# Port-aware ordering of an attention front, residual norms moved to ScalarE, and half sums, in a cross-attention and expert-FFN kernel

## The chip, the cores and the metric

The kernel runs on one core of one Trainium2 chip. The metric is the device time of one launch in microseconds; the shown time is the median of three runs. A profile of one execution comes with it. Engines are named as the profile names them: PE is TensorE, PEld its weight loads, DVE is VectorE, ACT is ScalarE, POOL is GpSimd and SP is SyncE, which here only issues DMAs.

## The reference, cut to what matters

Sixteen sequences of 112 tokens and 256 features (x) attend to sixteen contexts of 375 rows (ctx), all in float32. After the attention's residual comes a mixture of eight experts in which every token goes through every expert.

```python
x = x + xattn(layernorm(x), ctx, Wq, bq, Wk, bk, Wv, bv)
x = x + ffn(layernorm(x), w_router, w_gating, w_gate, w_up, w_down)

def xattn(t, c, ...):                       # one head, 256 wide
    q, k, v = t @ Wq + bq, c @ Wk + bk, c @ Wv + bv
    return softmax(q @ k.T / 16) @ v

def ffn(h, ...):                            # 8 experts, 256 -> 1024 -> 256
    cw = softmax(h @ w_router) * softmax(h @ w_gating / 0.1)
    cw = cw / (cw.sum(-1) + 1e-9)
    return sum(cw[e] * ((silu(h @ w_gate[e]) * (h @ w_up[e])) @ w_down[e]) for e in range(8))
```

## The kernel before, in words

**The front.** x arrives in four groups of four batches (`load_x`), ctx batch by batch (`load_ctx`). Wq and Wk are joined into one 256 by 256 matrix (`turned`, `joined`), and the biases are folded in as a column `r_sb`, a row `v_b` and a number `bqk_b` (`dotted`, L711, and `key_bias`, L720). For that, bq, bk and bv are loaded as rows repeated over 128 partitions (`row`, L627), and bk once more as columns (`columns`, L631), which VectorE widens into `bkb` (L730). Each group of x is normed (`stats` L751 and L752, a power on GpSimd at L759, `norm` at L771 or L776), transposed and multiplied with the joined matrix.

Each of the sixteen batches then runs a chain (`batch`): transposes of ctx (L846) and their copies out of PSUM (L853), scores (L858), maximum and shift (L866, L869), exponential (L873), transposes of the probabilities (L879) and copy (L884), mix of ctx rows (L892), a split into a high and a low part (L898, L901), projection by Wv (L907), residual (L914), then statistics of the new row x1 (L930 to L932), a power on GpSimd (L936), the residual norm x1n on VectorE (L942), its transposes (L950) and the copy into x1T (L957). When x1T of a half (eight batches, h = 0 or 1) is there, the router's logits follow (`route`, L978 to L1018), and the blocks that the FFN's products need.

**The FFN.** A step is an expert, a half of the tokens, one of four column blocks and gate or up: 128 steps. Each product of 2 x 2 blocks is made with seven block products instead of eight (`PROD`), each in three passes over high and low parts of both operands. So each half of x1T is needed as A11, A12, A22 and the sums S1 to S4 (`sum_x`, L256, on VectorE), each split by ScalarE into a rounded part (`split_hi`, L264) and by GpSimd or VectorE into the rest (`split_lo`, L267). The sums of both halves use the same buffer `sx`. The weights go the same way: `load_t` on GpSimd (L301 to L304), `load_hi` on ScalarE (L316), `load_lo` on GpSimd (L322). The down products (L383) fill gaps between block products (L417).

**What sets the order.** The engines run their instructions in the order of emission. For the front that order comes from a list, class `Line`: each operation is given with its engine, an assumed cost, a priority, what it reads and writes, and the buffers it takes. `run` simulates the engines by these costs, always takes the operation that can begin first (among equal ones the one of lower priority number), and emits all in the order of the simulated times. An operation is bound to one engine, and the list knows nothing of engines that hinder each other. The FFN's steps are written out by hand (`step`), with places where waiting pieces may be put in (`offer`). For h = 1 the four sums and five splits are such pieces, put into steps 1 to 3 by `sums_later`, two of the five rests on VectorE; the routing of h = 1 lies wholly in the list. Before the first data arrive, `idle` issues `WARM` = 11 matmuls on zeros.

**Memory.** Buffers of the FFN (`buf`) lie in one pool in the order of their first use; all have sizes that are multiples of 256 bytes.

Of the kernel before, what the change touches and what calls it, by code (L numbers as in the profile page):

```python
# [30 lines left out]
class Line:  # L31


    LAG = {"PE": 0.2, "SP": 0.1}

# [8 lines left out]
    def op(self, eng, cost, pri, emit, reads=(), writes=(), new=(), waits=(), kb=0):  # L44
        n = len(self.ops)
        deps = set()
        for k in reads:
            deps.update(self.writers[k])
        for k in waits:
            deps.update(self.uses[k])  # L50
        writes = tuple(writes) + tuple(x[1] for x in new)
        for k in tuple(reads) + writes:
            self.uses.setdefault(k, []).append(n)
        for k in writes:
            self.writers.setdefault(k, []).append(n)
        self.ops.append((eng, cost, pri, emit, deps, tuple(new), kb))
        return n

    def run(self):
        ops = self.ops  # L60
        end = {}
        free = {}
# [25 lines left out]
        while left:  # L88
            ready = {}
            for n in left:  # L90
                eng, cost, pri, emit, deps, new, kb = ops[n]
                if any(d not in end for d in deps):
                    continue
                t = max((end[d] + (0.0 if ops[d][0] == eng else self.LAG.get(ops[d][0], 0.1)) for d in deps), default=0.0)
                homes = {}
                for ring, key, *tag in new:
                    r, home = room(ring, tag[0] if tag else None, max(t, free.get(eng, 0.0)) - 0.1)
                    if r is None:
                        t = None
                        break  # L100
                    t = max(t, r + 0.1 if r else r)
                    homes[key] = home
                if t is not None:
                    ready.setdefault(eng, []).append((t, pri, n, homes))
            best = None
            for eng, c in ready.items():
                at = max(free.get(eng, 0.0), min(x[0] for x in c))
                x = min((x for x in c if x[0] <= at + 0.02), key=lambda x: (x[1], x[2]))
                if best is None or at < best[0]:
                    best = (at, eng, x)  # L110
            assert best, [(n, ops[n][0], ops[n][5]) for n in sorted(left) if all(d in end for d in ops[n][4])]
            at, eng, (_, _, n, homes) = best
            cost, kb, new = ops[n][1], ops[n][6], ops[n][5]
# [3 lines left out]
            free[eng] = at + cost  # L117
            end[n] = at + cost
# [5 lines left out]
        for at, n in sorted(line):  # L124
            ops[n][3]()
# [4 lines left out]
def kernel(  # L130
# [63 lines left out]

    def buf(tag, shape, name, dtype=F32):
        return fpool.tile(shape, dtype, tag=tag, name=name, bufs=BUFS[tag])
# [9 lines left out]
    nc.scalar.activation(warm, nhalf, AF.Exp)  # L206
# [33 lines left out]
    bk_c = spool.tile([P, KC], F32, tag="bk_c", name="bk_c", bufs=1)  # L240
    junk = cpool.tile([P, D], F32, name="junk")
# [6 lines left out]
    def sum_x(h, i):  # L248

        a11, a12, a21, a22 = blocks_of_x(h, 0, N)  # L250
        s1, s2, s3, s4 = (sx[:, k, :] for k in range(4))
        o, u, v, op = {
            X_S1: (s1, a21, a22, ALU.add), X_S2: (s2, s1, a11, ALU.subtract),
            X_S3: (s3, a11, a21, ALU.subtract), X_S4: (s4, a12, s2, ALU.subtract),
        }[i]
        nc.vector.tensor_tensor(o, u, v, op=op)  # L256

    def block_x(h, i):
        a11, a12, a21, a22 = blocks_of_x(h, 0, N)
        blocks = {X_A11: a11, X_A12: a12, X_A22: a22}  # L260
        return blocks[i] if i in blocks else sx[:, i - X_S1, :]

    def split_hi(h, i):
        nc.scalar.copy(xs_hi[h][i], block_x(h, i))  # L264

    def split_lo(h, i, eng):
        eng.tensor_sub(xs_lo[h][i], block_x(h, i), f(xs_hi[h][i]))  # L267
# [336 lines left out]

    def bank(key, shape):
# [14 lines left out]
    rsx, nmx, rs1, cs = (many(n, B) for n in ("rsx", "nmx", "rs1", "cs"))  # L620
# [5 lines left out]
    def row(t, v):  # L626
        nc.sync.dma_start(t, v.rearrange("(o d) -> o d", o=1).to_broadcast([P, D]))  # L627

    def columns():
        with nc.allow_non_contiguous_dma(reason="bias columns"):  # L630
            nc.sync.dma_start(bk_c, bk.rearrange("(c p) -> p c", p=P))  # L631
# [17 lines left out]

    def x_loaded(g):  # L650
        op("SP", 0.45, 4 * g - 6 if g else -22, lambda: load_x(g), new=(("xg", ("xg", g)),), kb=448)
# [4 lines left out]
    WARM = 11  # L656
# [9 lines left out]
    load(-18, 256, lambda: weight(nc.sync, wn[:, 1], Wk), "wn1")  # L666
    ctx_loaded(0)
    load(-3.2, 128, lambda: row(b_b[:, 0], bq), "bq")
    load(-3.1, 1, columns, "bkc")
    load(-3.0, 128, lambda: row(b_b[:, 1], bk), "bk")  # L670
    load(-2.0, 128, lambda: row(bv_b, bv), "bv")
    load(-1.7, 256, lambda: weight(nc.sync, wv, Wv), "wv")
    load(1.0, 16, load_router, "wr")
    for b in range(1, B):
        ctx_loaded(b)
    for g in range(1, B // G):
        x_loaded(g)

# [30 lines left out]
    def dotted(u, v, out, key, *reads):  # L709
# [6 lines left out]
        op("DVE", 0.52, -4, dot, reads=reads, writes=(key,))  # L716
# [11 lines left out]
    for i in range(KC):  # L728
        joined(i)
    op("DVE", 0.3, -8, lambda: nc.vector.tensor_copy(bkb, bk_c.unsqueeze(2).to_broadcast([P, KC, P])),  # L730
       reads=("bkc",), writes=("bkb",))
# [11 lines left out]
    def group(g):  # L743
# [10 lines left out]
        for i in range(G):  # L754
            op("DVE", 0.62, pri, lambda i=i: stats(i), reads=(("xg", g),), writes=(("st", g),))
        op("DVE", 0.18, pri, lambda: nc.vector.tensor_scalar_add(rsx[:TQ, at], mvx[:TQ, at, 1], EPS),
           reads=(("st", g),), writes=(("va", g),))
        op("POOL", 1.04, pri,
           lambda: nc.gpsimd.tensor_tensor(rsx[:TQ, at], rsx[:TQ, at], nhalf[:TQ, :G], op=ALU.pow),  # L759
           reads=(("va", g),), writes=(("rs", g),))  # L760
        op("DVE", 0.22, pri,
           lambda: nc.vector.scalar_tensor_tensor(
               nmx[:TQ, at], mvx[:TQ, at, 0], -1.0, rsx[:TQ, at], op0=ALU.mult, op1=ALU.mult),
           reads=(("rs", g),), writes=(("nm", g),))
# [16 lines left out]
        for i in range(G):  # L781
            key = ("xn", g, i // 2)
            op("DVE" if g == 0 and i % 2 else "ACT", 0.43, pri, lambda i=i: norm(i), reads=(("nm", g), ("xg", g)) + ((key,) if i % 2 else (("xnd", g if i else g - 1),) if g + i else ()),
               writes=((key,) if i % 2 else ()) + (("xnd", g),), new=(() if i % 2 else (("tt", key),)))
# [12 lines left out]
        for k in range(KC):  # L797
            op("PE", 0.4, pri, lambda k=k: turn(k), reads=(("xn", g, 0), ("xn", g, 1)),
               new=(("bank", ("xT", g, k)),))
            op("ACT", 0.54, pri, lambda k=k: nc.scalar.copy(xnT_b[k], bank(("xT", g, k), [P, GT])),  # L800
# [25 lines left out]
        for i in range(G):  # L826
            op("DVE", 0.52, pri + 0.5, lambda i=i: bias(i), reads=(("xn", g, i // 2), "v"), writes=(("c0", g),))
# [4 lines left out]
    def batch(b):  # L832
# [18 lines left out]
        for k in range(KC):  # L851
            op("PE", 0.33, b + 0.6, lambda k=k: turn(k), reads=(("ctx", b),), new=(("bank", ("cT", b, k)),))
            op("ACT", 0.45, b + 0.6, lambda k=k: nc.scalar.copy(ctT(k), bank(("cT", b, k), [P, TK])),  # L853
               reads=(("cT", b, k),), new=(("ctT", ("ctT", b, k)),))

        def score():
# [14 lines left out]
           reads=(("mx", b), ("c", g)), writes=(("nb", b),))  # L871
# [12 lines left out]
        op("ACT", 0.45, b, lambda: nc.scalar.copy(pT(), bank(("pp", b), [KT, NK, TQ])),  # L884
# [13 lines left out]
        op("ACT", 0.36, b, lambda: nc.scalar.copy(aT()[:, 0], bank(("aa", b), [P, KC, TQ])),  # L898
# [30 lines left out]
        def stats():  # L929
            nc.vector.bn_stats(st1[:TQ, b, :], x1())  # L930
            nc.vector.bn_aggr(mv1[:TQ, b, :], st1[:TQ, b, :])
            nc.vector.tensor_scalar_add(rs1[:TQ, col], mv1[:TQ, b, 1:2], EPS)  # L932

        op("DVE", 0.8, b, stats, reads=(("x1", b),), writes=(("va1", b),))
# [5 lines left out]
        def norm():  # L940
            t[0] = buf("y", [TQ, D], f"x1n{b}")
            nc.vector.tensor_scalar(  # L942
                t[0], x1(), mv1[:TQ, b, 0:1], rs1[:TQ, col], op0=ALU.subtract, op1=ALU.mult
            )

        op("DVE", 0.42, b, norm, reads=(("x1", b), ("rs1", b)), new=(("x1n", ("x1n", b)),))

        def turn_x1():
# [7 lines left out]
        op("ACT", 0.36, b,  # L956
           lambda: nc.scalar.copy(x1T[h][:, :, at * TQ : (at + 1) * TQ], bank(("xx", b), [P, KC, TQ])),  # L957
# [6 lines left out]

    lgs = [spool.tile([P, NTT, 2, E], F32, tag=f"lg{h}", name=f"lg{h}", bufs=1) for h in range(NH)]
# [4 lines left out]
    def route(h):  # L970
# [50 lines left out]

        op("DVE", 0.5, pri + 12, sums, reads=(("le", h),), writes=(("w1", h),))
# [4 lines left out]
    def split(h, i, pri, *reads):  # L1027
        op("ACT", 0.57, pri, lambda: split_hi(h, i), reads=reads, writes=(("xh", h, i),))
        op("POOL", 1.12, pri, lambda: split_lo(h, i, GP), reads=(("xh", h, i),) + reads, writes=(("xs", h, i),))
# [7 lines left out]
    for n, i in enumerate((X_S1, X_S2, X_S3, X_S4)):  # L1037
        op("DVE", 0.63, 9.5 + 0.1 * n, lambda i=i: sum_x(0, i),
           reads=early(0) + late(0) + [("sx", k) for k in (X_S1, X_S2, X_S3, X_S4)[:n]], writes=(("sx", i),))
    for i in (X_S2, X_S1, X_S3, X_A22, X_S4):  # L1040
        split(0, i, 10.5, *late(0), *([("sx", i)] if i != X_A22 else []))
    route(1)

# [90 lines left out]
    def sums_later():  # L1134
        for i in (X_S1, X_S2, X_S3, X_S4):
            sum_x(1, i)
            yield
        for i in (X_S2, X_S1, X_S3, X_A22, X_S4):
            split_hi(1, i)
            yield  # L1140
            split_lo(1, i, V if i in (X_S1, X_S2) else GP)
            yield

    for n in range(1, len(steps)):
        if n == 1:
            waiting.append(sums_later())
        assert not (waiting and n == 4)
        step(n)
    KEEP = 0
# [42 lines left out]
```

## Time and profile before

| | |
|---|---|
| median of 3 runs | 1007.76 us (1007.69 to 1008.76) |
| profiled execution | 1007.49 us, span 1005.7 us, 16283 instructions |
| busy PE, PEld | 981.5 us (98%), 911.1 us (91%) |
| busy DVE, ACT, POOL | 807.0 us (80%), 497.9 us (50%), 416.0 us (41%) |
| mean granted TensorE clock | 0.993 |
| DMA | 39.06 MB, mean 39 GB/s; 236 GB/s in the first 40 us |

The span is the time from the program's first to its last instruction; the execution's own time is some 2 us longer. A busy TensorE is not one at its peak, since its matmuls are pipelined. Windows of the span are counted in microseconds from its start.

### The profile page before, as it was taken

The numbers are of one execution on the slowest core, as the hardware profiler recorded it, in microseconds if no ns is written. First come the engines' busy times: TensorE is split into PE (matmuls) and PEld (weight loads), VectorE is DVE, ScalarE is ACT, GpSimd is POOL, SyncE is SP. The second block draws the span as 40 slices with busy tenths as digits, with TensorE's granted clock in tenths as the row PEclk, the third lists the DMA queues.
The fourth block names the chain that finished last, engine by engine and source line by source line (L and its number), as shares of the span: only waits on it lengthen the run. The fifth ranks groups of instructions, "written<-read, shape, count | busy, mean of one in ns | idle before, by whom it ended". The sixth has DMA issues, their size and how long they took to land.

```text
span 1005.7 us, 16283 instructions
## 1 busy us (share of the span) xinstructions
PE 981.5 (98%) x6055; PEld 911.1 (91%) x6055; DVE 807.0 (80%) x1481; ACT 497.9 (50%) x1017; POOL 416.0 (41%) x516
## 2 busy tenths in 40 slices
PE   8998879999999999999999999999999999999998
PEld 5777868999999999999999999999999999999998
DVE  6686689878878888878887887888887888788786
ACT  5565365445535554545544553555444544455342
POOL 4354456244605552356324460555235632455000
PEclk9998999999999999999999999999999999999999
DMA  8610101001100110011100110011001110010011
GB/s 233 184 55 21 45 22 53 22 23 43 53 1 22 43 42 22 11 43 42 34 11 23 43 53 1 22 43 43 22 12 42 43 32 11 22 43 1 1 37 37
DMA packets 36735, 39.06 MB, mean 39 GB/s; under 512 B 3552, under 2 KB 34656, under 8 KB 36656
## 3 DMA queue, kind: packets, MB, share of 16 engines
q1 hardware_dynamic: 36384, 37.76, 12.7%
q8 instruction: 47, 0.77, 0.3%
q14 instruction: 32, 0.26, 0.1%
q10 hardware_dynamic: 272, 0.26, 0.1%
HBM read 34.34 MB, written 1.84 MB: 36 GB/s over the span
## 4 chain that ended last, share of the span: by engine, by line
PE 91%; DVE 4%; DMA 2%; issue 1%; POOL 1%; ACT 0%; DVEq 0%; POOLq 0%; ACTq 0%
PE pd L383 31%; PE pC L417 15%; PE pA L417 15%; PE pB L417 15%; PE pE L417 7%; PE ps_aa L892 2%; PE ps_sc L858 2%; DMA ctx<-in_ctx_dram 1%; DVE x1n L942 1%; PE ps_po L907 1%; PE ps_cT L846 1%; PE ps_pp L879 0%; DMA wide<-in_x_dram 0%; PE ps_lg L978 0%; POOL rs L936 0%
## 5 line engine op out<-in xcount | busy, mean ns | idle before, releaser
L383 PE MATMUL pd<-wd,hhi 128*128 128x256 f32 x1792 | 340.7, 281 | 0.0
L383 PEld LDWEIGHTS pd<-wd,hhi 128*128 128x128 f32 x1792 | 309.6, 188 | 15.0
L383 PE MATMUL pd<-wd,hlo 128*128 128x256 f32 x896 | 253.1, 283 | 1.3 <-DVE hlo L470 0.7
L417 PE MATMUL pC<-xs_hi,w 128*128 128x448 f32 x508 | 188.6, 371 | 2.9 <-DVE s_4c L551 1.2
L417 PE MATMUL pB<-xs_hi,w 128*128 128x448 f32 x508 | 187.1, 368 | 2.7 <-DVE s_1w L528 2.7
L417 PE MATMUL pA<-xs_hi,w 128*128 128x448 f32 x504 | 186.8, 371 | 0.6 <-ACT v L523 0.6
L383 PEld LDWEIGHTS pd<-wd,hlo 128*128 128x128 f32 x896 | 169.5, 189 | 1.7 <-DVE hlo L470 0.9
L400 POOL TENSOR_TENSOR acc<-acc,y 128x256 f32<-128x256 f32 x45 | 36.0, 828 | 250.1 <-ACT y L399 250.1
L322 POOL TENSOR_TENSOR w<-raw,w 128x384 fp32r<-128x384 f32 x64 | 73.0, 1140 | 148.7 <-ACT w L316 148.7
L523 ACT COPY v<-pA 128x448 f32<-128x448 f32 x126 | 67.0, 532 | 91.6 <-PE pA L417 91.6
L417 PEld LDWEIGHTS pC<-xs_hi,w 128*128 128x128 f32 x508 | 96.1, 189 | 12.5 <-DVE s_4c L551 1.4
L417 PEld LDWEIGHTS pB<-xs_hi,w 128*128 128x128 f32 x508 | 96.0, 189 | 9.4 <-DVE s_1w L528 3.0
L417 PEld LDWEIGHTS pA<-xs_hi,w 128*128 128x128 f32 x504 | 95.6, 190 | 6.0 <-ACT v L523 0.9
L417 PE MATMUL pA<-xs_lo,w 128*128 128x448 f32 x252 | 92.6, 367 | 0.0
L417 PE MATMUL pC<-xs_lo,w 128*128 128x448 f32 x254 | 92.5, 364 | 0.0
L417 PE MATMUL pE<-xs_hi,w 128*128 128x448 f32 x254 | 92.4, 364 | 0.0
L417 PE MATMUL pB<-xs_lo,w 128*128 128x448 f32 x254 | 92.0, 362 | 0.0
L322 POOL TENSOR_TENSOR w<-tt,w 128x512 fp32r<-128x512 f32 x64 | 83.8, 1309 | 2.8
L331 POOL TENSOR_TENSOR wd<-rawd,wd 128x512 fp32r<-128x512 f32 x32 | 42.1, 1316 | 68.5 <-ACT wd L329 68.4
L417 PEld LDWEIGHTS pE<-xs_hi,w 128*128 128x128 f32 x254 | 47.7, 188 | 4.7
L417 PEld LDWEIGHTS pB<-xs_lo,w 128*128 128x128 f32 x254 | 48.4, 190 | 2.2
L417 PEld LDWEIGHTS pC<-xs_lo,w 128*128 128x128 f32 x254 | 48.3, 190 | 2.0
(1795 smaller groups left out, 1889.0 us busy)
## 6 DMA issues: line engine op xcount, KB each, us to landing
raw<-in_L_ffn_w_gate_dram SPq DMA_DIRECT2D x32, 256.0 KB
raw<-in_L_ffn_w_up_dram SPq DMA_DIRECT2D x32, 256.0 KB
rawd<-in_L_ffn_w_down_dram SPq DMA_DIRECT2D x32, 256.0 KB
ctx<-in_ctx_dram SPq DMA_DIRECT2D x13, 336.0 KB
wide<-in_x_dram SPq DMA_DIRECT2D x4, 448.0 KB
out_dram<-acc SPq DMA_DIRECT2D x6, 256.0 KB
wide<-in_ctx_dram SPq DMA_DIRECT2D x3, 336.0 KB
ctx<-in_ctx_dram SPq DMA_DIRECT2D x13, 39.0 KB
```

The costliest lines, as they stand in the source:

```text
L322: nc.gpsimd.tensor_sub(wts[k][1][:, d], w, f(wts[k][0][:, d]))
L331: nc.gpsimd.tensor_sub(wds[q][1], rawds[q], f(wds[q][0]))
L383: nc.tensor.matmul(pd, hs[a][:, t * P : (t + 1) * P], wds[q][w][:, fi, :], start=(opening and s == 0), stop=(last and s == 2), skip_group_ ...
L400: nc.gpsimd.tensor_add(acc[tt], acc[tt], y)
L417: nc.tensor.matmul(ps, w_[w][:, wi, :], (xs_hi, xs_lo)[a][h][xi], start=(start and s == 0), stop=(stop and s == 2), skip_group_check=True,)
L523: nc.scalar.copy(v1, pa)
L846: nc.tensor.transpose(bank(("cT", b, k), [P, TK])[:, c * KT : (c + 1) * KT], ct()[:, c, k * P : (k + 1) * P], ident[:KT, :KT],)
L858: nc.tensor.matmul(bank(("sc", b), [TQ, TK]), own(qk_b[k], ("qk", g, k))[:, i * TQ : (i + 1) * TQ], ctT(k), start=(k == 0), stop=(k == KC ...
L892: nc.tensor.matmul(bank(("aa", b), [P, KC, TQ])[:, k, :], ct()[:, c, k * P : (k + 1) * P], pT()[:, c, :], start=(c == 0), stop=(c == NK - 1),)
L907: nc.tensor.matmul(bank(("po", b), [TQ, D]), aT()[:, a, k, :], (wv_hi, wv_lo)[w][:, k, :], start=(k == 0 and s == 0), stop=(k == KC - 1 an ...
L942: nc.vector.tensor_scalar(t[0], x1(), mv1[:TQ, b, 0:1], rs1[:TQ, col], op0=ALU.subtract, op1=ALU.mult)
```

## The change

It has seven parts.

1. The list knows that GpSimd's operations and those of VectorE marked `port=True` exclude each other, and plans them one after the other.
2. An operation of the list may name several engines; the list takes the one that can begin first, the second with a handicap of 0.5 us. So the copies out of PSUM at L800, L853, L884, L898 and L957 go to ScalarE or VectorE.
3. The residual norm x1n goes from VectorE to ScalarE, as one ACTIVATE with a bias and a scale per row; the bias is made by one more small operation on each of VectorE and ScalarE.
4. The biases are loaded as one row each, on ScalarE's queue, and spread over the partitions by a matmul with ones; `bkb` comes from transposes. The first group of x is loaded and normed in two parts. ctx 1 is loaded ahead of Wv. The exponential's table is loaded after ScalarE's DMA issues, and there are 7 idle matmuls instead of 11.
5. For h = 1 the sums and splits are made in two parts: columns 0 to 223 in the list, the rest in steps 1, 2 and 4, with all `split_lo` on GpSimd.
6. The last four parts of the routing of h = 1 go from the list to steps 7 to 10.
7. Free words are put ahead of the buffers w (16), d (16), hhi (48) and hlo (32 words of 4 bytes); `junk` now shares memory with an accumulator.

```diff
+    SECOND = 0.5
...
-    def op(self, eng, cost, pri, emit, reads=(), writes=(), new=(), waits=(), kb=0):
+    def op(self, eng, cost, pri, emit, reads=(), writes=(), new=(), waits=(), kb=0, port=False):
...
+                    if t is not None:
+                        if port:
+                            t = max(t, free.get("port", 0.0))
+                        if e != engs[0]:
+                            t += self.SECOND
+                        ready.setdefault(e, []).append((t, pri, n, homes, cost))
...
+            if port:
+                free["port"] = at + cost
...
+    AHEAD = {"w": 16, "d": 16, "hhi": 48, "hlo": 32}
+
     def buf(tag, shape, name, dtype=F32):
+        if tag in AHEAD:
+            fpool.tile([P, AHEAD.pop(tag)], F32, tag=f"ahead_{tag}", name=f"ahead_{tag}", bufs=1)
...
+    EITHER = ("ACT", "DVE")
...
-    def row(t, v):
-        nc.sync.dma_start(t, v.rearrange("(o d) -> o d", o=1).to_broadcast([P, D]))
+    def row(queue, t, v):
+        queue.dma_start(t[:1], v.rearrange("(o d) -> o d", o=1))
...
-    WARM = 11
+    WARM = 7
...
+    def spread(name, t, pri):
+        k = ("b", name)
+        op("PE", 0.45, pri, lambda: nc.tensor.matmul(bank(k, [P, D]), ones, t[:1], start=True, stop=True),
+           reads=(name + "0",), new=(("bank", k),))
+        op("ACT", 0.38, pri, lambda: nc.scalar.copy(t, bank(k, [P, D])), reads=(k,), writes=(name,))
...
-            op("ACT", 0.45, b + 0.6, lambda k=k: nc.scalar.copy(ctT(k), bank(("cT", b, k), [P, TK])),
+            op(EITHER, (0.45, 0.53), b + 0.6, lambda e, k=k: copy_on(e, ctT(k), bank(("cT", b, k), [P, TK])),
...
+            nc.vector.tensor_scalar_mul(nm1[:TQ, col], mv1[:TQ, b, 0:1], -1.0)
...
-            nc.vector.tensor_scalar(
-                t[0], x1(), mv1[:TQ, b, 0:1], rs1[:TQ, col], op0=ALU.subtract, op1=ALU.mult
+            nc.scalar.activation(
+                t[0], x1(), AF.Identity, bias=nm1[:TQ, col], scale=rs1[:TQ, col]
             )
...
-        op("DVE", 0.42, b, norm, reads=(("x1", b), ("rs1", b)), new=(("x1n", ("x1n", b)),))
+        op("ACT", 0.2, b - 0.5,
+           lambda: nc.scalar.activation(nm1[:TQ, col], nm1[:TQ, col], AF.Copy, scale=rs1[:TQ, col]),
+           reads=(("rs1", b),), writes=(("nm1", b),))
+        op("ACT", 0.55, b - 0.5, norm, reads=(("x1", b), ("nm1", b)), new=(("x1n", ("x1n", b)),))
...
+        if h:
+            tail.extend((sums, shares, rest, weights))
+            return
...
+    M = N // 2
...
+    for n, i in enumerate(SUMS):
+        op("DVE", 0.36, 29 + 0.1 * n, lambda i=i: sum_x(1, i, 0, M),
+           reads=there + [("sx1", k) for k in SUMS[:n]] + [("xs", 0, k) for k in SUMS], writes=(("sx1", i),),
+           port=True)
+    for i in (X_A22, X_S1, X_S2, X_S3, X_S4):
+        of = there + ([("sx1", i)] if i != X_A22 else [])
+        op("ACT", 0.37, 29, lambda i=i: split_hi(1, i, 0, M), reads=of, writes=(("xh1", i),))
+        op("POOL", 0.62, 29, lambda i=i: split_lo(1, i, 0, M), reads=[("xh1", i)] + of, writes=(("xs1", i),))
...
-    def sums_later():
...
+    REST = {
+        1: [later(sum_x, X_S1), later(split_hi, X_A22), later(split_hi, X_S1), later(sum_x, X_S2),
+            later(split_lo, X_A22, X_S1), later(split_hi, X_S2)],
+        2: [later(sum_x, X_S3), later(split_lo, X_S2), later(split_hi, X_S3), later(sum_x, X_S4),
+            later(split_hi, X_S4)],
+        4: [later(split_lo, X_S3), later(split_lo, X_S4)],
+        7: tail[:1], 8: tail[1:2], 9: tail[2:3], 10: tail[3:],
+    }
```

## The prediction

> **What bounds the kernel now.** I read the page's slices first, then its groups, then the windows of the front, the timeline and waits inside the bad windows. The slices say where to look: TensorE is at 9 tenths in every slice from the seventh on, so what it lacks lies in the first six, the front (0 to about 145 us) and its seam.
>
> ```profile
> PE   8998879999999999999999999999999999999998
> PEclk9998999999999999999999999999999999999999
> ```
>
> A slice is 25 us. From 150 us on TensorE is the bound: a step is 7 products of 3 matmuls at about 0.205 us from start to start plus 7 down groups of 3 at 0.1186 us, 6.8 us, and 128 steps make 868 us. Nothing in the diff removes a matmul there. What can move is the front, and its windows (columns: length, then busy of PE, PEld, DVE, ACT, POOL, then granted clock, DMA share and GB/s) show where TensorE has no work:
>
> ```profile
> 60.00:75.00 15.00, 14.88 (x114) 12.94 (x112) 12.51 (x36) 9.03 (x23) 10.35 (x16) 1.00 0.11 33
> 75.00:85.00 10.00, 5.46 (x26) 5.13 (x26) 7.60 (x11) 3.46 (x11) 5.57 (x6) 0.66 0.01 2
> 85.00:100.00 15.00, 15.00 (x103) 12.45 (x102) 8.99 (x30) 9.58 (x26) 5.13 (x8) 1.00 0.09 28
> 100.00:110.00 10.00, 7.50 (x47) 6.74 (x46) 7.00 (x11) 4.89 (x13) 5.69 (x7) 0.83 0.29 86
> 110.00:122.00 12.00, 12.00 (x91) 11.11 (x90) 6.97 (x21) 4.57 (x13) 3.24 (x4) 1.00 0.07 19
> 122.00:145.00 23.00, 18.09 (x85) 14.46 (x84) 19.80 (x43) 14.28 (x30) 10.10 (x14) 0.93 0.06 17
> ```
>
> Windows 75 to 85 and 100 to 110 are idle and at a reduced clock; 122 to 145 has VectorE at 86%. The timeline names the first stall (the last column is idle time and its releaser):
>
> ```profile
> 75.03 3.31 POOL L267 TENSOR_TENSOR xs_lo<-sx,xs_hi 128x448 fp32r<-128x448 f32 x3
> 75.09 4.49 DVE L942 TENSOR_SCALAR x1n<-wide,mv,rs 112x256 f32<-112x256 f32 x1 [0.44 <-POOL rs L936]
> 78.31 1.12 POOL L267 TENSOR_TENSOR xs_lo<-wide,xs_hi 128x448 fp32r<-128x448 f32 x1
> 79.50 0.26 DVE L993 TENSOR_REDUCE lmx<-lg 128x14 f32<-128x112 f32 x1
> ```
>
> A residual norm that takes 0.40 us alone took 4.49 us: it started 0.06 us after GpSimd and ended when GpSimd's four subtractions ended. The group of all sixteen, and the waits of TensorE at the front's end:
>
> ```profile
> L942 DVE TENSOR_SCALAR x1n<-wide,mv,rs 112x256 f32<-112x256 f32 x16 | 18.2, 1136 | 3.9 <-POOL rs L936 3.8
> ```
>
> ```profile
> PE pB L417 <- DVE s_1w L528: 2.7, 1, 2.7
> PE pC L417 <- DVE s_4c L551: 1.2, 1, 1.2
> PE pC L417 <- DVE s_1c L551: 0.8, 1, 0.8
> PE pC L417 <- DVE s_3c L551: 0.8, 1, 0.8
> PE pd L383 <- DVE hlo L470: 0.7, 1, 0.7
> ```
>
> **What the Trainium skill says.** "SBUF — State Buffer", Who interferes with whom: VectorE and GpSimd share a port pair as an exclusive lock, and a VectorE `tensor_scalar` from SBUF to SBUF can want it while ScalarE never waits. The trace agrees: 4.49 us against 0.40. "TensorE: Matmul & The Clock Gate", Part 1: after an idle window the array runs at half clock for a while. Agreed: after the 4.54 us gap 21 transposes took 4.30 us, 0.205 each against 0.107. "ScalarE: Activation LUTs" puts an ACTIVATE at 186 ns plus 0.833 ns an element plus 93 ns per pointer operand, 0.585 us for 256 columns with two; the group L776 here has 0.599.
>
> **The change, part by part.**
>
> (a) Residual norms. Sixteen x1n leave VectorE (18.2 us busy, of which 16 x 0.405 = 6.5 is work and 11.7 blocking). Added: a VectorE multiply by -1 in `stats` (0.08 us, like the small ones at L886 and below), an ACTIVATE on 112x1 (186 + 93 = 0.28 us, estimate from the ScalarE page) and a norm of 0.60 us (row L776). Per batch the way from x1 to x1n grows by 0.08 + 0.28 + 0.60 - 0.41 = 0.55 us; ScalarE gains 14 us in a front where it is busy 67 of the first 122 us. What TensorE lost to these norms: idle 4.54 at 79.6, 2.50 at 104.4, about 0.65 at 54.6, 1.15 at 41.2, together 8.8 us; then half clock: in 79.6 to 84.4 about 2.4 us (21 transposes 2.1, ps_xx 0.3), in 104.8 to 108.3 about 1.7 us (L892 x12 in 2.40 instead of 1.33, L907 x6 in 1.30 instead of 0.72). That is 12.9 us. The power on GpSimd (L936, 0.55 us) stays behind whatever GpSimd is doing (at 74.13 it had waited 2.4 us for eight tt subtractions), so I don't credit all: 10 us, ends 5 and 13.
>
> (b) The list knows ports, evictions on either engine. 88 evictions (cT 32, pp, aa and xx 16 each, xT 8) may go to VectorE at 0.4 to 0.6 us (L737, PSUM to SBUF with 256 columns, 0.41). This removes small waits of TensorE on ScalarE and VectorE (0.45 at 35.5, 0.51 at 58.5) and keeps x1n's queue on ScalarE short. Credit 0.5; the ordering itself I can't price, it is in the ends of (a).
>
> (c) The end of the front. VectorE loses from 126 to 139 us: the eight routing operations L1005 to L1018, 1.81 us, moved to steps 7 to 10, where a step has 6.8 us and VectorE is busy 5.6; two subtractions L267 at 0.63 (1.26), which go to GpSimd; of the four sums L256 (0.62, 0.62, 1.01, 0.87, together 3.1) half the columns go ahead into the stretch 110 to 122, where VectorE is busy 58%. A half sum costs 224 columns, about 0.38 us by 0.62 less 224/448 of its 0.47 us of columns. So 4.7 us leave the stretch in which TensorE waits 7.4 us (2.7 + 1.2 + 0.8 + 0.8 + 0.7 + 0.6 on hlo L477 + 0.6 on ACT v) and runs 3.4 us at half clock after the 2.7 us gap (1.7 us lost). The longest wait goes: s_1w had both inputs at 126.4 and ran at 130.15, behind routing and sums. Credit 5 of 9.1, ends 2 and 8. The ten half conversions of ScalarE and GpSimd (0.37 and 0.62) lie beside it. Late next: Silu's table load, 1.28 us at 126.98.
>
> (d) The start. The first x comes in two halves, so stats begin perhaps 0.7 us earlier and the norms of a pair no longer wait for four stats (2.2 us) and a 1.03 us power; the broadcasts of three biases (3 x 128 KB) and the 4-byte column load leave the DMA queues, 384 KB at the 230 to 270 GB/s of the windows, 1.5 us of wire; SP issues four transfers fewer (0.40 to 0.68 each) and two more for x and an earlier ctx. Added on TensorE: three spreads (the four matmuls of L698 take 1.99 us, so 0.50 each) and two transposes (0.26), 1.8 us, on ScalarE four copies of 0.38, covered by the wait for Wq until 6.37 and for xT until 12.95; if biases land after Wq they push the weight chain by 1.8 us, which has some 2 of room (the second m_sb was there at 10.2, xT began at 12.95). Four warm-up matmuls go (4 x 0.43): if the clock then falls, up to 2 us. Credit 1.5, ends -1.5 (loss) and 3.
>
> (e) Free words ahead. They move the start of four buffer families by 64 to 192 bytes. The six matmuls of L907 read weights at 448-byte steps, several such phases, and still take 0.72 us for six in the chain, the pace of the down groups; the two halves of x sit at different addresses and step alike. Cost 0; bound 1 ns either way on 5376 matmuls, 5.4 us.
>
> (f) New waits: x1n is now ahead of evictions in ScalarE's order; when its power is late, an exponential or a copy behind it is late. I charge 1.5 us, ends 0 and 26 (the rival).
>
> Sum: -10 - 0.5 - 5 - 1.5 + 0 + 1.5 = -15.5. The profiled execution took 1007.49 us (span 1005.7 and 1.8 around it), 0.27 below the median of the runs: 992.0 and about 992.3; I say 992.
>
> **Rivals.**
>
> Half of it: the wait turns into one on the power at GpSimd. For: L936 already waited up to 2.4 us behind tt and the two ACTIVATEs lengthen the way. Against: L936's other waits are for VectorE. Then (a) is 5, (c) 2: 1007.5 - 5 - 2 - 1 + 1 = 1000.5.
>
> The layout helps: matmuls lose 1.5 ns each; 992 - 8 = 984. Against: no phase shows in L907.
>
> Slower: ScalarE's queue is in order, and each norm blocks the evictions behind it until the power is done. Place: the four bursts of GpSimd work as at 70 to 79 us, each 4.4 us, and then about 2 us of half clock: 4 x 6.4 = 26, less the 17 of gain: 1016. It decides from 17/16 = 1.06 us of TensorE wait per batch on. Against: ScalarE is half idle and the list now counts GpSimd's bursts.
>
> It does nothing: the gaps are refilled by others of the same length, 1007.
>
> **How the numbers follow.** 0.2% (2 us) is about what a measurement of this kernel can tell from no change. The main case 0.62 (985 to 999 of its own), half 0.19, layout 0.06, nothing 0.03, slower 0.10. Faster 0.87, within 0.03, slower 0.10. The range 983 to 1004 leaves out the slower case, "nothing" and the best part of the layout case, some 0.17.
>
> **What would show it.** Right: no x1n on VectorE, sixteen on ScalarE at 0.6 us; no TensorE wait over 2 us on ps_xx; clock 1.00 from 20 to 145 us; ps_second begins near 112 instead of 123.3 us; s_1w not behind routing; the step still 6.8 us. Wrong: ScalarE waiting for rs L936 for over 1 us a batch; TensorE waiting for ScalarE's copies; matmul spacing off 0.205 and 0.1186; a half-clock stretch at 6 to 12 us.

## The result, and the profile after

The changed kernel takes 990.04 us, median of 4 runs (988.84 to 990.98), against 1008.0 of the kernel before in the same job: a ratio of 0.982 (0.9803 to 0.9837). The forecast was 992.0. The profiled execution has a span of 989.0 us against 1005.7, 16.7 less.

The page's slices of the kernel after, of TensorE and its clock, in tenths of 25 us each:

```profile
PE   9999879999999999999999999999999999999998
PEclk9999999999999999999999999999999999999999
```

The first and the fourth slice, 8 before, are now 9; the longest stall of a norm lay in the fourth. The fifth and sixth, 8 and 7, are as they were. The windows of the kernel after (length, busy PE, PEld, DVE, ACT, POOL, then clock, DMA share, GB/s) say the same in finer steps:

```profile
60.00:75.00 15.00, 15.00 (x112) 13.01 (x111) 11.64 (x40) 10.71 (x30) 6.67 (x11) 1.00 0.09 26
75.00:85.00 10.00, 9.11 (x56) 6.83 (x55) 8.70 (x22) 5.97 (x17) 6.66 (x9) 1.00 0.01 2
95.00:105.00 10.00, 7.74 (x54) 6.25 (x53) 9.77 (x17) 5.99 (x16) 6.62 (x7) 1.00 0.24 70
105.00:122.00 17.00, 15.38 (x96) 13.92 (x95) 10.68 (x32) 10.03 (x27) 6.47 (x12) 0.90 0.08 21
122.00:145.00 23.00, 18.10 (x93) 14.72 (x92) 20.64 (x30) 14.21 (x31) 18.78 (x22) 1.00 0.16 46
```

In 75 to 85 us TensorE has 9.11 us busy at full clock, where it had 5.46 at 0.66. In 122 to 145 it is not busier (18.10 after 18.09), but it runs 93 matmuls instead of 85. From 95 to 105 us TensorE is still busy for only 7.74 of 10 us (7.50 before), and VectorE now for 9.77 (8.10 before). Past the first 13 us one half-clock stretch is left, at 118.3 to 121.7.

The norms, from the view of one tile (min, median and max in ns), and TensorE's longest waits. In these lines `pA` to `pE` are the accumulators of the FFN's block products, `pd` that of the down products, `s` and `v` in the FFN sums of products on their way to the hidden values (in the front `s` holds copies out of PSUM), and `hhi` and `hlo` the rounded part and the rest of the hidden values:

```profile
L1008 ACT ACTIVATE x1n<-wide,nm,rs x16: 599/601/603, 33.2 to 116.7; 112x256 f32<-112x256 f32 x16
```

```profile
PE ps_sc L923 <- DVE s L628: 2.3, 2, 1.4
PE pd L402 <- DVE hlo L489: 1.7, 1, 1.7
PE ps_pp L944 <- ACT s L938: 0.9, 1, 0.9
PE pC L436 <- DVE s_1c L570: 0.8, 1, 0.8
```

No norm is blocked any more, and the wait of 2.7 us for `s_1w` is gone. The first line is two waits for copies out of PSUM that part 2 gave to VectorE. The longest single wait is now 1.7 us, for `hlo` on VectorE at 130.5 us, in a stretch where VectorE is busy with sums without a pause.

So far this is the forecast. But the place of the gain is not. I split the two traces at fixed points of the work (us from the span's start; a projection's time is the start of its last matmul, a step's that of its first product into pA):

| | before | after | difference |
|---|---|---|---|
| first transpose of x (ps_xT) | 12.95 | 14.93 | +2.0 |
| projection of batch 0 | 28.80 | 30.48 | +1.7 |
| projection of batch 15 | 120.88 | 113.75 | -7.1 |
| step 8 | 178.93 | 169.82 | -9.1 |
| step 20 | 260.45 | 250.58 | -9.9 |
| step 127 | 987.43 | 971.10 | -16.3 |

The start lost 2 us in this execution. The front up to step 8 gained 9.1 us, not the 15.5 of the forecast's sum. From step 20 to step 127 the same 107 steps took 726.98 us before and 720.52 after: 6.794 and 6.734 us a step, where I had forecast no change. The windows from 300 to 900 us show it as a count. Before, then after:

```profile
300.00:900.00 600.00, 600.00 (x3711) 568.49 (x3710) 491.86 (x840) 297.97 (x587) 263.40 (x325) 1.00 0.10 30
```

```profile
300.00:900.00 600.00, 600.00 (x3743) 571.51 (x3742) 496.53 (x849) 300.76 (x592) 266.89 (x333) 1.00 0.10 30
```

TensorE is busy for all 600 us in both, at full clock in both, and does 3743 matmuls instead of 3711, 0.9% more. Idle time can't explain that, since the profile shows none: the matmuls themselves come faster. The page's groups show which. Before, then after (busy us, mean ns of one):

```profile
L383 PE MATMUL pd<-wd,hlo 128*128 128x256 f32 x896 | 253.1, 283 | 1.3 <-DVE hlo L470 0.7
L417 PE MATMUL pA<-xs_hi,w 128*128 128x448 f32 x504 | 186.8, 371 | 0.6 <-ACT v L523 0.6
```

```profile
L402 PE MATMUL pd<-wd,hlo 128*128 128x256 f32 x896 | 250.8, 280 | 1.7 <-DVE hlo L489 1.7
L436 PE MATMUL pA<-xs_hi,w 128*128 128x448 f32 x504 | 183.0, 363 | 0.0
```

A record's length overlaps its neighbours', so I took the mean distance from one start to the next (200 to 960 us, ns, before and after): pA from xs_hi 207.9 and 201.3, pA from xs_lo 205.4 and 197.9, pd from hlo 118.9 and 117.5, pC from xs_hi 208.0 and 206.6. Of the others, pE from xs_lo falls by 2.2 but comes once a step, and the rest move by 1 or less, some of them up. By the numbers of each in a step (4, 2, 7 and 4) the four make 26 + 15 + 10 + 6 = 57 ns of the step's 60.

The theory for the experiments: two parts carry the gain, the place of the norms (front) and the free words (the whole FFN). The rivals: the matmuls come faster for another reason (`split_lo` all on GpSimd, a clock that differs); or the front's gain comes from the list's knowledge of ports, or from the end of the front, and the norm's engine doesn't matter.

### The profile page after: what moved, and what is told of

Read it like the earlier page. It is cut to its first block, busy times and chain, and to the rows that moved or that the text cites. A ratio compares the mean times of both kernels' runs of the same rounds, so it can differ in the third digit from the quotient of the medians.

```text
span 989.0 us, 16353 instructions
## 1 busy us (share of the span) xinstructions
PE 972.8 (98%) x6059; PEld 907.4 (92%) x6059; DVE 804.3 (81%) x1506; ACT 504.7 (51%) x1037; POOL 415.7 (42%) x524
## 4 chain that ended last, share of the span: by engine, by line
PE 94%; DVE 3%; ACT 1%; issue 1%; DMA 0%; POOL 0%; DVEq 0%
PE pd L402 32%; PE pC L436 16%; PE pB L436 15%; PE pA L436 15%; PE pE L436 8%; PE ps_aa L957 2%; PE ps_sc L923 2%; PE ps_qk L869 1%; PE ps_po L972 1%; PE ps_cT L911 1%; PE ps_pp L944 0%; DVE low L934 0%; DMA wn<-in_L_xattn_Wq_dram 0%; PE ps_lg L1048 0%; PE ps_xT L856 0%
## 5 line engine op out<-in xcount | busy, mean ns | idle before, releaser
L436 PE MATMUL pA<-xs_hi,w 128*128 128x448 f32 x504 | 183.0, 363 | 0.0
```

The lines of the kernel that those rows point to most:

```text
L436: nc.tensor.matmul(ps, w_[w][:, wi, :], (xs_hi, xs_lo)[a][h][xi], start=(start and s == 0), stop=(stop and s == 2), skip_group_check=True,)
```

## The experiments

Each kernel ran against the kernel before on one chip, whose median in these jobs was 1007.1 to 1007.9 us.

**Does the layout alone do it?** e1 is the kernel before with the addresses of the kernel after and nothing else:

```diff
+    AHEAD = {"w": 16, "d": 16, "hhi": 48, "hlo": 32}
...
+        if tag in AHEAD:
+            fpool.tile([P, AHEAD.pop(tag)], F32, tag=f"ahead_{tag}", name=f"ahead_{tag}", bufs=1)
...
+    cpool.tile([P, P], F32, name="as_ones")
-    junk = cpool.tile([P, D], F32, name="junk")
+    junk = acc[-1]
-    rsx, nmx, rs1, cs = (many(n, B) for n in ("rsx", "nmx", "rs1", "cs"))
+    rsx, nmx, rs1, _, cs = (many(n, B) for n in ("rsx", "nmx", "rs1", "as_nm1", "cs"))
```

> The kernel before with the addresses of the changed one: the free words ahead of w, d, hhi and hlo, a pad in the place of ones and of nm1, junk in the accumulator. Nothing else differs. Theory of the forecast (the layout costs nothing): 1007.8, within 2 us. Rival, from the two traces (step 8 to the end is 819.2 us after and 826.8 before): the layout alone carries the steady part, 1000 to 1001 us, with step 20 to 127 taking 720.5 instead of 727.0 us.

Measured: 1001.26 us, ratio 0.9936 (0.9915 to 0.9958). Step 8 begins at 179.34 (before: 178.93), and steps 20 to 127 take 720.64 us, as in the kernel after. Its window from 300 to 900 us:

```profile
300.00:900.00 600.00, 600.00 (x3744) 571.52 (x3743) 496.05 (x849) 302.92 (x597) 266.81 (x330) 1.00 0.10 30
```

e2 is the reverse, the kernel after with w, d, hhi, hlo and the rest back at multiples of 256 bytes:

```diff
-    AHEAD = {"w": 16, "d": 16, "hhi": 48, "hlo": 32}
+    AHEAD = {"y": 48}
```

> The changed kernel with 48 free words ahead of y alone, so that w, hhi, hlo, s and d begin at multiples of 256 bytes as before and x's blocks at 192 past one as before. Theory of the forecast: 990.0. Rival: 997 to 998, step 20 to 127 back at 727 us, the front as in the changed kernel.

Measured: 997.12 us, ratio 0.9896 (0.9878 to 0.9913). Step 8 begins at 169.68 (after: 169.82), and steps 20 to 127 take 727.10 us, as before:

```profile
300.00:900.00 600.00, 600.00 (x3708) 568.42 (x3707) 492.11 (x841) 298.66 (x588) 265.84 (x329) 1.00 0.10 30
```

3711 and 3708 matmuls with the old addresses, 3743 and 3744 with the new: the whole difference in the steady part is the buffers' place in memory, and it leaves the front alone. e1 keeps the old order and the old `split_lo`, and the clock is full in all four windows, so neither of these is the cause. It is worth 5.8 us in the one kernel and 7.1 in the other by the medians, 6.3 and 6.6 by the steps 20 to 127.

**Which buffer?** Modulo 256 bytes, as the built programs place them, the old addresses are: xs 192; w, hhi, hlo, the sums s and v, and d 0. The new ones are: xs 192, w 128, hhi 64, hlo and s and v 192, d 0. l1 moves w alone, l2 all but w:

```diff
-    AHEAD = {"w": 16, "d": 16, "hhi": 48, "hlo": 32}
+    AHEAD = {"y": 48, "w": 32, "hhi": 32}               # l1: only w, at 128
+    AHEAD = {"y": 48, "hhi": 16, "hlo": 32, "d": 16}    # l2: hhi at 64, hlo, s and v at 192
```

> The changed kernel with only the FFN weights w at their new place in 256 bytes (128 past a multiple), while hhi, hlo, s, v1 and d begin at multiples of 256 as in the kernel before. If what counts is where w lies against x's blocks (192): most of the layout's 7 us stays, step 20 to 127 in 720 to 722 us, 990 to 992. If it is the hidden parts and the temporaries: 726 to 727 us, 996 to 997.

> The complement: hhi at 64, hlo, s and v1 at 192 as in the changed kernel, w and d at multiples of 256. If it is w against x: step 20 to 127 in 726 to 727 us, 996 to 997, with at most 1.5 us of gain from the down groups' hlo. If it is the hidden parts and temporaries: 720 to 722 us, 990 to 992.

Measured: l1 993.9 us (0.9863, 0.9847 to 0.9879), l2 990.2 us (0.9831, 0.9814 to 0.9848). Steps 20 to 127 take 723.75 us in l1 and 721.72 in l2: of the 6.5 us, w alone gives 3.3 and the others alone 5.3, together not their sum. So it isn't one buffer alone that lay badly. Nor is it only a matter of a matmul's own operands: in l2 xs and w keep their old places within 256 bytes, and yet pA from xs_lo, whose neighbours in TensorE's order are products of xs and w too, falls from 205.4 to 200.8 ns from start to start (203.2 in l1, 197.9 in the kernel after). Which accesses get in each other's way stays open.

**Is the lost start the warm-up?** e3 has 11 idle matmuls again, and nothing else:

```diff
-        for _ in range(WARM):
+        for _ in range(11):
```

> The changed kernel with 11 idle matmuls instead of 7, the list's plan left as it is. If the four matmuls that were taken away keep the clock at half until 12.5 us and the first transposes and joins are on the path of the front: 2 to 3 us faster, 987 to 988, clock at full from about 6 us and xT near 13 instead of 14.9 us. Rival (the start is bound by the landing of x and Wq, and four more matmuls only push the weights' transposes): 990 to 991.5.

Measured: 990.02 us (0.9828, 0.9813 to 0.9843), no difference. The clock is full from 6.33 to 9.75 us and half from there to 13.16, and the first transpose of x comes at 14.67, 0.26 earlier. The three spreads run there at full clock, in 0.59 to 0.69 us each instead of 1.05 to 1.22, and that brings next to nothing: the four matmuls more move the first transpose of Wq from 5.00 to 5.85 us, and the half-clock stretch falls on the eight matmuls that join Wq and Wk, 3.27 us instead of 2.35. More warm-up matmuls do not win the start back.

**The norms.** e5 is the kernel before with only the residual norm on ScalarE, the addresses of the FFN's buffers unchanged:

```diff
+            nc.vector.tensor_scalar_mul(nm1[:TQ, col], mv1[:TQ, b, 0:1], -1.0)
...
-            nc.vector.tensor_scalar(
-                t[0], x1(), mv1[:TQ, b, 0:1], rs1[:TQ, col], op0=ALU.subtract, op1=ALU.mult
+            nc.scalar.activation(
+                t[0], x1(), AF.Identity, bias=nm1[:TQ, col], scale=rs1[:TQ, col]
...
-        op("DVE", 0.42, b, norm, reads=(("x1", b), ("rs1", b)), new=(("x1n", ("x1n", b)),))
+        op("ACT", 0.2, b - 0.5,
+           lambda: nc.scalar.activation(nm1[:TQ, col], nm1[:TQ, col], AF.Copy, scale=rs1[:TQ, col]),
+           reads=(("rs1", b),), writes=(("nm1", b),))
+        op("ACT", 0.55, b - 0.5, norm, reads=(("x1", b), ("nm1", b)), new=(("x1n", ("x1n", b)),))
```

> The kernel before with only the residual norm moved to ScalarE (the multiply by -1, the small operation and the ACTIVATE of the change, at the change's list costs); the list knows no ports, all buffers stay at their addresses. Theory of the forecast (blocked norms are what the front loses): 8 to 10 us faster than before, 997 to 999. Rival, after the run with the norm back on VectorE was not slower (a good order is what counts): the rest of the order stays blind, other operations that need the port and the end of the front still stall, 1002 to 1007.

Measured: 998.55 us (0.9902, 0.9887 to 0.9917), 9.2 us less. Step 8 begins at 169.97, 8.96 earlier; steps 20 to 127 take 727.15. The front's window from 60 to 122 us, before and then e5:

```profile
60.00:122.00 62.00, 54.85 (x375) 48.37 (x374) 43.07 (x108) 31.53 (x84) 29.98 (x39) 0.92 0.11 33
```

```profile
60.00:122.00 62.00, 58.53 (x388) 49.58 (x388) 42.47 (x126) 42.70 (x111) 30.88 (x43) 0.94 0.12 35
```

ScalarE takes 11 us more, TensorE is busy 3.7 us longer and is further in its work. The half-clock stretches at 77.5 and 104.8 us are gone; one at 114.5 to 121.3 has come.

e4 is the kernel after with the norm back on VectorE, in a list that still knows that GpSimd can hold it up:

```diff
-        op("ACT", 0.2, b - 0.5,
-           lambda: nc.scalar.activation(nm1[:TQ, col], nm1[:TQ, col], AF.Copy, scale=rs1[:TQ, col]),
-           reads=(("rs1", b),), writes=(("nm1", b),))
-        op("ACT", 0.55, b - 0.5, norm, reads=(("x1", b), ("nm1", b)), new=(("x1n", ("x1n", b)),))
+        op("DVE", 0.42, b, norm, reads=(("x1", b), ("rs1", b)), new=(("x1n", ("x1n", b)),), port=True)
```

> The changed kernel with the residual norm back on VectorE, as an operation that the list knows to need the shared port (its cost in the list 0.42, no multiply by -1, no small operation on ScalarE). Theory of the forecast (the norm on ScalarE carries the largest part): 5 to 9 us slower, 995 to 999, with x1n blocked for over 1 us several times. Rival (a list that knows the port plans round the collisions, so that the engine matters little): 990 to 992.

Measured: 987.37 us (0.9804, 0.9786 to 0.9822). It is not slower than the kernel after but 2.7 us faster by the medians, though the intervals of the two overlap. The sixteen norms there, in the view of one tile:

```profile
L1007 DVE TENSOR_SCALAR x1n<-wide,mv,rs x16: 383/408/1277, 33.4 to 114.9; 112x256 f32<-112x256 f32 x16
```

TensorE still waits 3.5 us for norms there, 2.69 of them at 115.8 us for the last one (0.85 us long), and the clock is at half from 116.4 to 123.2 us.

e6 is e4 with a list that knows nothing of ports:

```diff
-        self.ops.append((eng, cost, pri, emit, deps, tuple(new), kb, port or eng == ("POOL",)))
+        self.ops.append((eng, cost, pri, emit, deps, tuple(new), kb, False))
```

> The changed kernel with the norm back on VectorE, as in the run before, and a list that knows of no shared port: the exclusion is taken out for all operations. If the list's knowledge of the port stands in for moving the norm: 5 to 9 us slower than with it, 993 to 997, with x1n blocked up to 3 us as in the kernel before. Rival (the other parts shift the work apart anyway): 987 to 990.

Measured: 990.41 us (0.9818, 0.9798 to 0.9838). One norm was caught for over 1 us, as the timeline of e6 shows (start, length, engine, what it did, and the idle time with its releaser):

```profile
92.29 1.01 POOL L341 TENSOR_TENSOR w<-raw,w 128x384 fp32r<-128x384 f32 x1
92.35 4.48 DVE L1007 TENSOR_SCALAR x1n<-wide,mv,rs 112x256 f32<-112x256 f32 x1 [0.66 <-POOL rs L1001]
...
95.42 1.26 POOL L341 TENSOR_TENSOR w<-tt,w 128x512 fp32r<-128x512 f32 x1
...
96.89 0.41 PE L1015 MATMUL ps_xx<-ident,x1n 112*128 112x112 f32 x2 [3.47 <-DVE x1n L1007]
```

The norm began 0.06 us after GpSimd's first conversion and ended with the last of a row of them; TensorE waited 3.47 us for it. This is the pattern of the kernel before, where five norms took over 1 us. So the other parts of the change alone, with neither the move nor the port knowledge, already leave only one. Without port knowledge the longest norm takes 4.48 us, with it 1.28. In time that is 3.0 us by the medians (1.1 at step 8), but the intervals overlap, so this size is not settled.

**The end of the front.** e8 is the kernel after with the routing of h = 1 back in the list, and the sums and splits whole, in steps 1, 2 and 4:

```diff
-        if h:
-            tail.extend((sums, shares, rest, weights))
-            return
...
-    for n, i in enumerate(SUMS):
-        op("DVE", 0.36, 29 + 0.1 * n, lambda i=i: sum_x(1, i, 0, M),
...
-        return lambda: [what(1, i, M, N) for i in blocks]
+        return lambda: [what(1, i, 0, N) for i in blocks]
```

> The changed kernel with the routing of h = 1 wholly in the list again and its sums and splits made whole in steps 1, 2 and 4 (all rests on GpSimd). Theory of the forecast (this relief of VectorE at the end of the front is worth 5 us): 994 to 996. Rival, from the landmarks of the two traces (from the last projection to step 8 the change is only 2.0 us shorter, 56.1 instead of 58.1): 991 to 993.

Measured: 993.58 us (0.9849, 0.9832 to 0.9865), 3.5 us more than the kernel after; step 8 begins 2.5 us later, of which 0.4 is there already at the first transpose of x.

**Evictions.** e7 leaves all 88 copies out of PSUM on ScalarE. In the kernel after, 21 of them went to VectorE, 15 of them those of ctx.

```diff
-    EITHER = ("ACT", "DVE")
+    EITHER = ("ACT",)
```

> The changed kernel with all 88 copies out of PSUM on ScalarE alone. If the freedom of engine carries part of the front's 9 us, as relief of a ScalarE that has the norms too: 2 to 4 us slower, 992 to 994. Rival, from the trace after (in VectorE's order a copy that waited 2.4 us for transposes stood ahead of nmx at 12.3 us, and copies on VectorE end TensorE's waits at 78.5 and 97.2): 987 to 990.

Measured: 991.19 us (0.9824, 0.9804 to 0.9843): 1.2 us more by the medians, within the intervals. The first transpose of x comes at 13.27 there, 1.7 earlier than in the kernel after, and this is gone again by batch 15 (114.17 after 113.75).

**Why the start is late.** It looks as if a copy of ctx on VectorE did it, since in the kernel after VectorE stands before one for 2.36 us, with a norm of x behind it:

```profile
11.80 0.55 DVE L628 COPY s<-ps_cT 128x375 f32<-128x375 f32 x1 [2.36 <-PE ps_cT L911]
12.27 0.15 DVE L817 SCALAR_TENSOR_TENSOR nmx<-mvx,rsx 112x2 f32<-112x2 f32 x1
12.33 0.41 DVE L826 TENSOR_SCALAR xn<-wide,mvx,rsx 112x256 f32<-112x256 f32 x1
```

But TensorE does not wait for that norm. Its own timeline shows no idle time that counts (an idle time would stand in brackets):

```profile
6.12 1.22 PE L714 MATMUL ps_b_bq<-b_b,ones 1*128 1x256 f32 x2
7.13 1.05 PE L714 MATMUL ps_b_bk<-b_b,ones 1*128 1x256 f32 x2
7.98 1.06 PE L714 MATMUL ps_b_bv<-mix,ones 1*128 1x256 f32 x2
...
10.30 1.46 PE L911 MATMUL ps_cT<-ident,ctx 125*128 125x125 f32 x6
11.56 2.35 PE L749 MATMUL ps_m<-wT 128*128 128x256 f32 x8
```

From the first transpose of Wq at 5.00 to the first transpose of x at 14.93 us it is busy for 9.90 us and idle for 0.04. In the kernel before the same stretch, from 6.37 to 12.95, holds 5.23 us of work. So the start is late because TensorE has more work to do in it, most of it at half clock: here the clock comes to full only at 12.47 us.

When the clock comes to full does not seem to be fixed by the program's order. e2, l1 and l2 have the order of the kernel after, copies on VectorE included. In e2 the clock is full at 13.13 and the first transpose of x comes at 15.02; in l1 and l2 it is full from 5.09 and 5.42 us for 3.4 us, and the transpose comes at 13.67 and 13.54. Of the eight profiled kernels with 7 idle matmuls three had the early clock, e7 among them (4.08 us); all six with 11 had it by 6.6 us. What the early clock wins is still there later: step 8 begins at 168.14 and 167.94 in l1 and l2, at 169.82 and 169.68 in the kernel after and e2. Against l1 and l2, which started alike, e7 is some 2 us late at step 8 (170.10), which speaks for the free engine. These are single executions, and a difference of 1 or 2 us between two variants can be that of their starts.

**Two parts alone.** e10 is the kernel before with e5's edit and e1's edit together: the norms on ScalarE and the new addresses, none of the other five parts.

> Two of the seven parts put on the kernel before: the residual norm on ScalarE, and the addresses of the changed kernel. If these two are the change's whole net gain (alone they took 9.2 and 5.8 to 6.5 us off) and their gains add up: 991.5 to 993, step 8 near 170.2 us and step 20 to 127 in 720 to 721. If the list's knowledge, the free engine, the new start and the half sums give net time beyond them: no better than the sum, and the changed kernel at 990 stays 2 us or more ahead. If the two share a gain: 995 to 998.

Measured: 990.47 us (0.9827, 0.981 to 0.9845), against 990.04 (0.9803 to 0.9837) of the whole change. Step 8 begins at 168.49, steps 20 to 127 take 720.70 us. Two of the seven parts make all of it, and alone they add up to nearly as much (9.2 and 5.8 against 17.5 together). The other five come out at nothing as a net: e8 shows that two of them are worth some 3 us inside the whole change, so that others should lose about as much; only for the start does a run show it (e9).

**A better version.** e9 is e4 with the start of the kernel before: rows broadcast by DMA, bk as columns, the first x whole, the exponential's table first, ctx 1 behind Wv, 11 idle matmuls.

```diff
-    WARM = 7
+    WARM = 11
...
-    def row(queue, t, v):
-        queue.dma_start(t[:1], v.rearrange("(o d) -> o d", o=1))
+    def row(t, v):
+        nc.sync.dma_start(t, v.rearrange("(o d) -> o d", o=1).to_broadcast([P, D]))
```

> The changed kernel with the residual norm on VectorE, known to the list as an operation of the shared port, and with the start of the kernel before: biases broadcast by DMA and bk as columns, the first group of x loaded and normed whole, the exponential's table first, ctx 1 behind Wv, 11 idle matmuls. Theory of the forecast (the new start is worth 1.5 us): 989. Rival, from the landmarks (xT begins at 15.5 us with the new start and at 12.95 with the old one, and the first projection 2.3 us later): 985 to 986, which would be below both kernels.

Measured: 986.54 us (986.14 to 987.15), ratio 0.9791 (0.9776 to 0.9806); all its runs lie below all those of the kernel after. The first transpose of x comes at 11.96 us, step 8 at 166.08, 2.2 us earlier than in e4, and the clock is full from 5.81 us to the end. Against e4 the medians differ by only 0.8 us. Two norms are caught there, for 2.45 and 1.55 us: a plan on assumed costs does not rule it out.

## Why the prediction was right and wrong

The total was right: 992.0 forecast, 990.04 measured, faster as expected. The sum behind it was not, and that it came out was luck. It put all 15.5 us in the front, which gave 9.1, and nothing in the steady part, which gave the rest.

- **Step (a), the norms, right.** Forecast 10, between 5 and 13; e5 measured 9.2 alone. That waits and half clock were both counted and then cut for the power on GpSimd was the right way to size it, though the wait at 41.2 us is 0.81 us in the trace, not 1.15. What I missed is that the engine isn't the point: the blocking depends on where the norm stands beside a burst of GpSimd. e4, which leaves the norm on VectorE but plans around the bursts, loses nothing, and e6, with neither, keeps only one long block. With the other parts in place the move brings no gain; the longer way from x1 to x1n and the fuller ScalarE would explain that, but no run shows it by itself.
- **Step (b), ports and evictions, undecided.** Credit 0.5; e7 gives 1.2 for the evictions inside the noise (2 at step 8 against runs that started alike), and the ports give 3.0 between e6 and e4, also inside it. In the kernel after the norm is no longer there to be caught.
- **Step (c), the end of the front, mis-sized.** Credit 5, measured 3.5 by the medians and 2.5 at step 8 (e8). `s_1w` is no longer held up, as said. The term that failed is what leaves VectorE. The half sums ran in 0.38 us where they were made ahead, but the four left in the steps took 0.38, 0.90, 0.64 and 0.65: 0.6 us of the 3.1 went, where some 1.5 was counted. VectorE remained at 20.64 of 23 us there, so that the next wait, `hlo` with 1.7 us, took a part of the credit. And of the 7.4 us of waits in the sum 2.6 lay after 146 us, outside the stretch that was relieved. I had named Silu's table load as the next to be late; it moved ahead to 120.6 and it was VectorE again.
- **Step (d), the start, wrong in sign.** Credit 1.5 gained; the front's first milestone came 2.0 us later, the projection of batch 0 1.7. The lower end of -1.5 was too tight. The step that failed is that TensorE's added work was covered, by the wait for Wq until 6.37 and for x until 12.95. Wq had landed at 4.86, the spreads and the transposes of bk came behind its first transposes and took 3.35 us of TensorE's chain where 1.8 was counted, and from there on TensorE had no wait to hide them in. The loss for a clock that falls was named, up to 2 us, but not charged: l1 and l2, with the early clock, are 1.3 and 1.4 us earlier at the first transpose of x, and 10.8 and 11.0 us ahead of the kernel before at step 8 instead of 9.1.
- **Step (e), the free words, wrong.** Forecast 0; measured 6.3 to 6.6 us on 107 steps. My two pieces of evidence didn't carry it. L907's six matmuls have operands of other sizes and no neighbour like those of the FFN. And the two halves of x lie a multiple of 256 bytes apart, so that they have the same phase and had to step alike. The bound of 1 ns on each matmul was far too small for some: pA's passes move by 6.6 and 7.5 ns, and the first of them after a down group by 11.0 (212.1 to 201.1). The rival that said so, 984, had the step right, and added it to a front that gave less.
- **Step (f), new waits, small.** Charged 1.5. The sixteen norms ran at 0.60 us and TensorE's longest wait for ScalarE was 0.9 us; the rival in which ScalarE's queue blocks, with 26 us, did not occur. Its price can't be told apart from e4's 2.7.

Of the signs, "the step still 6.8 us" was named for being right and failed (6.73), and "a half-clock stretch at 6 to 12 us" was named for being wrong and came. The errors cancelled. The front fell 6.4 us short of the sum in the profiled execution, and the layout brought some 6.5 of the 7.6 that came after step 8 and weren't in it. A slip without effect: 128 steps of 6.8 us are 870 us, not 868.

What the Trainium skill has on this: "SBUF — State Buffer", Who interferes with whom, states that only the shared port pair causes contention. The norms agree with it: 4.48 us in e6 behind GpSimd on VectorE, 0.60 on ScalarE in the kernel after. For the steady part it isn't enough: with an unchanged list of instructions, e1 changed the places of buffers within 256 bytes by 64 to 192, and the FFN's steps went from 6.794 to 6.735 us. The measurement decides.

Open stays which accesses collide in the old layout. That the distances of pA's first pass after a down group hardly differ from the 5th to the 95th percentile (209 to 214 ns before, 200 to 201 after) speaks for a regular cost in each such matmul and against chance meetings with other engines. In l1 and l2 they spread more, from 204 and 205 to 212. The runs don't show more.

## What to carry to other kernels

When a vector operation takes ten times its own time, see what the other engine was doing as it started: moving it to a third engine took the long stalls away here, and so did an order that keeps it off the bursts, which makes no chain longer. Before summing up gains in a front, compare one steady step too: in a kernel bound by TensorE a count of matmuls in a long window of equal busy time shows a change of pace that no wait shows. Work that is put on an engine "under a wait" is free only if that wait is still there after the change; and an idle time on one engine is no cause of a delay until the engine that is late is seen to wait for it. Where the clock of the first microseconds differs between executions, compare starts that had the same clock.

## What the hardware showed that I had not expected

The start address of a buffer within 256 bytes changes the pace of these block matmuls: the first pass into pA after a down group 212.1 to 201.1 ns from start to start, 3711 to 3743 matmuls in 600 us of a TensorE that is busy throughout. Moving only the weights gives half of it (3.3 of 6.5 us), moving only the other buffers four fifths (5.3), and with these a pass whose own operands had stayed went from 205.4 to 200.8 ns.

A VectorE operation that loses its turn to GpSimd waits for the whole row of GpSimd's operations that stand back to back, 4.48 us behind conversions of 1.0 to 1.3 us, not for the one that was running.

With the same 7 idle matmuls at its beginning TensorE had the full clock by 5.5 us in three of eight profiled kernels and only at 12.5 to 14.0 us in the five others.
